# An attention and feed-forward block: sixteen weight loads change queue, one read-back gets a condition, and a turn's tensor step is issued first

## The chip, the cores and the metric

The kernel runs on one core of one Trainium2 chip. The metric is the device time of one execution in microseconds (us). A core has five engines that work side by side, each through its own instructions in a fixed order, and they wait for one another through semaphores: TensorE (PE) multiplies matrices into PSUM, VectorE (DVE) and ScalarE (ACT) do elementwise work and reductions, GpSimd (POOL) does slower elementwise work, and SyncE (SP) mostly issues DMA transfers. A DMA is issued by one of SyncE, ScalarE or GpSimd, in the order of that engine's instructions; an issue that has to wait holds back everything behind it on the same engine.

## The reference

The input is x with 4 batches of 1024 tokens of 256 numbers. Attention has 16 heads of 16 numbers; then a gated feed-forward part with ternary weights follows. All is in 32-bit floats.

```python
q, k, v = split_heads(layernorm(x) @ Wqkv.T)          # 16 heads of 16
s = q @ k.T / sqrt(16)
e = exp(clip(s - max(s), -50, 50))
attn = e / (sum(e) + 1e-6)
x = x + layernorm((attn @ v) @ Wout.T)

h = silu(lin(layernorm(x), w1)) * lin(layernorm(x), w2)   # 256 -> 1024
h = gelu(lin(h, h1)); h = gelu(lin(h, h2))                # 1024 -> 1024
x = x + layernorm(lin(h, w3))                             # 1024 -> 256
```

The 1e-6 is added to a sum of exponentials that were taken relative to the row's maximum. A kernel that doesn't subtract the maximum first must therefore still know it: it adds 1e-6 times the largest exponential of the row.

## The kernel before

**Tiling of attention.** The 16 heads are taken in 4 groups of 4 (`g`), the 1024 queries in 2 halves of 512 (`h`), the 1024 keys in 8 chunks of 128 (`c`). A *unit* is one batch, group and half; there are 4 x 4 x 2 = 32 of them, one after the other. A unit has 8 chunks of 2 tiles (`u`, two heads each), so 512 tiles in all. For each tile TensorE makes the scores `s` (L534) from two stacked operands `sk` and `sq`, ScalarE takes the exponential into a buffer `e` (L535), and TensorE weighs the values `vaug` with it into `acc` (L542). The buffers `e` are a ring of 8 tiles, so that a new exponential overwrites one that must have been weighed, and looked at by VectorE.

**The maxima.** Along the way VectorE keeps, in `top`, the elementwise maximum over chunks of the exponentials of the first 128 queries (`rise`, L554). A query of that kind may have a sum so small that the 1e-6 counts. At a unit's end (`unit_end`) `acc` is transposed into `o` (L787, two buffers), and `divide` (L567 to L587) brings the maxima to the right place: `top` is sent to DRAM as `top_d` (L572), read back as `folded` (`back`, L575, one buffer), reduced by three VectorE instructions (`fold`, L579 and L580), and then `run` takes the last maximum (L584) and calls `quotients`, which divides (L561 to L565) and writes the result to `on`. `run` frees `folded`. For the first group of a later batch, `run` waits until the projection of the batch before has read the same `on`.

**The stacks.** A head group's operands are put together by 32 DMA copies of 64 KB (`stack` and `copies`, L482), 16 for `sk` and then 16 for `sq`, all from SyncE's queue, four in a step. Two groups of stacks exist; the copies for group g + 2 begin when group g has ended and have to land before group g + 1 has.

**Other transfers in attention.** `load_rest` (L218 to L234) lists what is loaded beside the first units: a part of x, then the output weights `wo_sb` in 16 pieces of 16 x 256 (16 KB), then the last batch's x and the scales, one per turn and all from SyncE's queue. The output weights are first read by the projection `py` at the end of batch 0. GpSimd rounds the feed-forward weights (`round_weights`, `round_corners`) with loads and stores on its own queue, copies the values into `vaug` (L512), and takes reciprocal square roots (`rstd`, L107).

**The planner.** The Python code that writes the program runs *turns*. In each, three tiles of scores and exponentials are issued, then maxima of complete chunks, then weighings, then more exponentials, and at the end `side.take`: that spends what is left of the turn on side work, which is the next batch's normalisation, transposes and projections, stack copies, divisions, the ends of batches, and loads. Side work stands in *chains* of `Step`s in `self.first` (divisions and batch ends) and `self.rest` (all else). A step has a gap in turns to its forerunner, a condition `ready`, and a flag `tensor` if it uses TensorE; at most one tensor step is issued in a turn. The order of issue in the turn is the order of the chains. A tensor step issues its matmuls and also the instructions that empty its PSUM tile: `to_vector` (L327), the second half of a projection (L394), `bound` (L426), or the splitting of a transposed input (L327 and L901). All of them write to one PSUM buffer, `misc`, so that the next tensor step's matmuls wait until the last one's tile has been emptied.

**Order on an engine.** What the Python code issues first is first on its engine; there is no reordering afterwards.

Of the kernel before, what the change touches and what calls it, by code (L numbers as in the profile page):

```python
# [21 lines left out]
DH = 16  # L22
# [21 lines left out]
@with_exitstack  # L44
def tile_attention_ffn_block(ctx: ExitStack, tc: tile.TileContext, x, wqk, wv, wo, w1, w1s, w2, w2s, h1, h1s, h2, h2s, w3, w3s, out):

    nc = tc.nc
    B, S, D = x.shape
    bad = ctx.enter_context(tc.tile_pool(name="flag", bufs=1)).tile([1, 1], I32, name="bad")
    tile_fast(tc, x, wqk, wv, wo, w1, w1s, w2, w2s, h1, h1s, h2, h2s, w3, w3s, out, bad)
    failed = nc.values_load(bad[0:1, 0:1], min_val=0, max_val=1 << 24)
    with tc.If(failed > 0):  # L70
        tile_general(tc, x, wqk, wv, wo, w1, w1s, w2, w2s, h1, h1s, h2, h2s, w3, w3s, out)
# [58 lines left out]
def tile_fast(ctx: ExitStack, tc: tile.TileContext, x, wqk, wv, wo, w1, w1s, w2, w2s, h1, h1s, h2, h2s, w3, w3s, out, bad):  # L130
    nc = tc.nc
# [25 lines left out]
    def load_x(b, halves=range(NH)):  # L157
        view = x[b].rearrange("(t p) d -> p t d", p=P)
        for h in halves:
            for at, tokens in pieces(h, view):  # L160
                nc.sync.dma_start(out=xs[b][:, at, :], in_=tokens)
# [34 lines left out]
    with ExitStack() as actx, ExitStack() as rctx:  # L196
# [4 lines left out]
        wo_sb = aw.tile([P, DC, D], F32, name="wo_sb")  # L201
# [16 lines left out]
        def load_rest():  # L218


            def load(out, in_):
                return lambda: nc.sync.dma_start(out=out, in_=in_)

            def load_half(b, h):
                return lambda: load_x(b, [h])

            rest = [load_half(2, h) for h in range(NH)]
            for c in range(DC):
                for h in range(HPT):
                    r = SLOT * (HPT * c + HPG * (h % GPT) + h // GPT)  # L230
                    rest.append(load(wo_sb[DH * h : DH * (h + 1), c, :], wo[r : r + DH, :]))
            rest += [load_half(b, h) for b in range(3, B) for h in range(NH)]
            rest += [load(scales[name], w) for name, w in (("w1", w1s), ("w2", w2s), ("h1", h1s), ("h2", h2s))]
            return rest + [load(w3s_sb, w3s.partition_broadcast(P))]  # L234
# [21 lines left out]
        work = actx.enter_context(tc.tile_pool(name="work", bufs=2, side="right"))  # L256
# [299 lines left out]
        def quotients(g, h, em, o):  # L556

            o = o.rearrange("p (j s) -> p j s", s=SLOT)
            den = small.tile([P, NQ // SLOT], F32, tag="den", name="den")
            n = P // SLOT  # L560
            nc.vector.scalar_tensor_tensor(den[:, 0:n], em, SM_EPS, o[:, 0:n, DH], ALU.mult, ALU.add)  # L561
            nc.vector.tensor_copy(den[:, n:], o[:, n:, DH])
            nc.vector.reciprocal(den, den)
            e = DH * (g % GPT)
            nc.vector.tensor_mul(on[h][:, g // GPT, :, e : e + DH], o[:, :, 0:DH], den.unsqueeze(2).to_broadcast([P, NQ // SLOT, DH]))  # L565

        def divide(g, h, o, top):  # L567


            there = shuffle.tile([HPG, P, P], F32, tag="top", name="top_d")  # L570
            folded = work.tile([P, P // SLOT, P], F32, tag="folded", name="folded", bufs=1)
            nc.sync.dma_start(out=there.rearrange("i k q -> k i q"), in_=top.rearrange("p u n q -> p (u n) q"))  # L572

            def back():
                nc.sync.dma_start(out=folded, in_=there.rearrange("i (k s) q -> (i k) s q", s=P // SLOT))  # L575

            def fold():
                for n in (2, 1):
                    nc.vector.tensor_max(folded[:, 0:n], folded[:, 0:n], folded[:, n : 2 * n])  # L579
                nc.vector.transpose(folded[:, 1], folded[:, 0])  # L580

            def run():
                em = small.tile([P, P // SLOT], F32, tag="em", name="em")
                nc.vector.tensor_reduce(em, folded[:, 1].rearrange("p (j k) -> p j k", k=SLOT), AX.X, ALU.max)  # L584
                quotients(g, h, em, o)

            return [Step(back, 2, False), Step(fold, 2, False, work=1.2), Step(run, 1, False, work=1.4)]  # L587

        def divide_last(g, h, o, top):

# [88 lines left out]
        class Side:  # L679
# [34 lines left out]
            def take(self, room=math.inf, spare=0.0):  # L714

                self.slot += 1
                free, heavy = True, False
                step = self.next_tensor(self.slot)

                self.room = min(self.room, 0.5) + room - (step.work if step and not step.heavy else 0)  # L720
                for chain in self.first + self.rest:
                    while (step := self.due(chain, self.slot, free)) and (step.tensor or not step.work or self.room > spare):
                        chain[0].pop(0)
                        chain[1] = self.slot
                        if step.split:
                            step.run(0)
                            chain[0].insert(0, Step(lambda run=step.run: run(1), 1, work=step.work))
                            self.open = chain
                        else:
                            if step.tensor and self.open is chain:  # L730
                                self.open = None
                            step.run()
                        free = free and not step.tensor
                        heavy = heavy or step.heavy
                        self.room -= 0 if step.tensor else step.work
                self.tired = heavy
# [47 lines left out]
        def unit_end(b, g, h):  # L784

            o = both.tile([P, NQ], F32, tag="o", name="o", bufs=2)
            nc.vector.transpose(o, accs[b, g, h])  # L787
            unit = side.add((divide_last if (b, g) == (B - 1, NG - 1) else divide)(g, h, o, tops[b, g, h]), True)
            if b and not g:

# [382 lines left out]
        class Checks:  # L1173
# [7 lines left out]
            def load(self):  # L1181
                k = self.loaded
                if k < min(len(self.blocks), self.seen + 2):
                    w, c, i = self.blocks[k]
                    self.st[k] = xs[0][:, TPQ * (k % 2) : TPQ * (k % 2 + 1), :].rearrange("p t d -> p (t d)")
                    nc.sync.dma_start(out=self.st[k].rearrange("p (i d) -> p i d", i=i), in_=w[c * P : (c + i) * P, :].rearrange("(i p) d -> p i d", p=P))
                    self.loaded += 1
# [156 lines left out]
        side.add(early + v[2:] + [Step(slots(0, 0), 0, False), Step(slots(0, 1), 0, False)] + sum(qk[1], []) + [Step(lambda: later.update(qk1=0, v=0), 0, False), Step(lambda: add_flags(flags[0] + flags[1]), 0, False)])  # L1344
        begin(0)
        side.add(stack(0, 1) + few(load_rest(), 1))
        side.add([s for k in blocks for s in round_weights(*k)] + [s for k in corners for s in round_corners(*k)])
        made = seen = weighed = half = 0
# [8 lines left out]
        while weighed < len(tiles):  # L1357
# [14 lines left out]
            while halves and weighed + 2 <= n:  # L1372
                b, g, h, c, _ = tiles[weighed]
# [264 lines left out]
```

## Time and profile before

Three runs took 1228.26, 1232.06 and 1233.94 us; the median is 1232.06.

| What | Value |
|---|---|
| Time of the profiled execution | 1232.08 us |
| Its span, first to last instruction | 1230.2 us |
| TensorE's mean granted clock over it | 0.987 |
| Attention stage, roughly | 0 to 592 us |
| TensorE busy in 30 to 600 us | 539.0 of 570 us |
| ScalarE busy in 30 to 600 us | 501.0 of 570 us |
| VectorE busy in 30 to 600 us | 402.4 of 570 us |
| GpSimd busy in 30 to 600 us | 173.4 of 570 us |
| DMA engines, mean share in 30 to 600 us | 0.62 |
| Exponentials (L535) | 512 of 1.043 us, 483.1 us |
| One maximum (L554) | 0.723 us |
| One load of `wo_sb`, issue to landing, median | 2.5 us |

How to read it: "busy" is the time in which an engine executes, "waits" are idle times of an engine, each put down to what ended it. The granted clock is the share of full speed that TensorE's clock was given. In a timeline each row has a start, a length, the work with its tiles (out<-in) and shape, how many instructions were merged into the row, and in brackets the idle time before it and its releaser. SPq rows are SyncE's queue; their length includes waiting in the issue.

### The profile page before, as it was taken

The numbers are of one execution on the slowest core, as the hardware profiler recorded it, in microseconds if no ns is written. First come the engines' busy times: TensorE is split into PE (matmuls) and PEld (weight loads), VectorE is DVE, ScalarE is ACT, GpSimd is POOL, SyncE is SP. The second block draws the span as 40 slices with busy tenths as digits, with TensorE's granted clock in tenths as the row PEclk, the third lists the DMA queues.
The fourth block names the chain that finished last, engine by engine and source line by source line (L and its number), as shares of the span: only waits on it lengthen the run. The fifth ranks groups of instructions, "written<-read, shape, count | busy, mean of one in ns | idle before, by whom it ended". The sixth has DMA issues, their size and how long they took to land.

```text
span 1230.2 us, 21266 instructions
## 1 busy us (share of the span) xinstructions
PE 1169.1 (95%) x7994; PEld 710.1 (58%) x7994; DVE 841.5 (68%) x1500; ACT 885.1 (72%) x1049; POOL 209.1 (17%) x279
## 2 busy tenths in 40 slices
PE   7999999999999999999999999999999999999993
PEld 2333333333333333333578888887888878888783
DVE  3485668777687756868685756867578676784755
ACT  3798899878988989999457565576656766566651
POOL 6222035434354432000000000000000000000000
PEclk8999999999999999999999999999999999999997
DMA  4676755756666666453314341344512545125401
GB/s 132 175 183 152 172 148 134 186 135 175 152 162 154 173 168 148 96 140 128 104 34 138 119 156 52 103 171 147 178 59 97 175 156 176 62 82 199 155 7 37
DMA packets 78672, 163.66 MB, mean 133 GB/s; under 512 B 14688, under 2 KB 40928, under 8 KB 78560
## 3 DMA queue, kind: packets, MB, share of 16 engines
q1 hardware_dynamic: 68624, 131.27, 38.7%
q0 software_dynamic: 9408, 30.42, 7.7%
q8 instruction: 65, 1.06, 0.4%
q10 hardware_dynamic: 528, 0.52, 0.2%
q14 instruction: 47, 0.39, 0.1%
HBM read 98.71 MB, written 29.88 MB: 105 GB/s over the span
## 4 chain that ended last, share of the span: by engine, by line
PE 58%; DVE 12%; ACT 12%; SPq 6%; DMA 6%; issue 5%; ACTq 0%; POOL 0%; POOLq 0%; DVEq 0%
PE ph L1034 27%; PE acc L542 9%; PE pg L955 8%; ACT e L535 6%; PE s L534 6%; SPq L482 5%; PE p L321 3%; DVE lo L929 2%; ACT hi L925 2%; PE py L321 2%; DVE top L554 1%; DMA sq<-cq1lo 1%; DMA folded<-top_d 1%; PE pz L1139 1%; DVE w L1045 1%
## 5 line engine op out<-in xcount | busy, mean ns | idle before, releaser
L535 ACT ACTIVATE e<-s 128x1024 f32<-128x1024 f32 x512 | 483.1, 1043 | 53.8 <-PE s L534 44.1
L542 PE MATMUL acc<-e,vaug 128*32 128x512 f32 (+1 forms) x2424 | 258.7, 539 | 2.9 <-POOL vaug L512 2.9
L534 PE MATMUL s<-sq,sk 64*128 64x512 f32 x1024 | 189.3, 446 | 25.3 <-ACT e L535 17.1
L534 PEld LDWEIGHTS s<-sq,sk 64*128 64x128 f32 x1024 | 87.6, 185 | 172.0 <-ACT e L535 142.1
L1034 PE MATMUL ph<-hi,sq 128*128 128x512 f32 x448 | 178.1, 398 | 0.8 <-DVE w L1045 0.8
L1034 PE MATMUL ph<-lo,sq 128*128 128x512 f32 x448 | 176.7, 394 | 0.0
L1034 PE MATMUL ph<-hi,sk 128*128 128x512 f32 x448 | 176.7, 394 | 0.0
L1034 PE MATMUL ph<-lo,sk 128*128 128x512 f32 x448 | 176.4, 394 | 0.0
L107 POOL TENSOR_TENSOR rstd<-ve,minus_half 128x4 f32<-128x4 f32 (+1 forms) x34 | 38.2, 1123 | 740.6 <-DVE ve L105 681.8
L554 DVE TENSOR_TENSOR top<-top,e 128x512 f32<-128x512 f32 x192 | 138.9, 723 | 24.3 <-ACT e L535 18.5
L542 PEld LDWEIGHTS acc<-e,vaug 128*32 128x32 f32 x2424 | 61.8, 109 | 120.5 <-issue 107.8
L929 DVE TENSOR_TENSOR lo<-c,hi 128x1024 fp32r<-128x1024 f32 x48 | 58.4, 1223 | 66.0 <-ACT hi L925 66.0
L929 DVE TENSOR_TENSOR lo<-g,hi 128x1024 fp32r<-128x1024 f32 x48 | 58.8, 1226 | 58.0 <-ACT hi L925 57.7
L1034 PEld LDWEIGHTS ph<-hi,sq 128*128 128x128 f32 x448 | 84.2, 188 | 21.6 <-DVE w L1045 2.1
L1034 PEld LDWEIGHTS ph<-hi,sk 128*128 128x128 f32 x448 | 84.1, 188 | 20.0
L1034 PEld LDWEIGHTS ph<-lo,sk 128*128 128x128 f32 x448 | 84.1, 188 | 19.9
L1034 PEld LDWEIGHTS ph<-lo,sq 128*128 128x128 f32 x448 | 84.2, 188 | 19.1
L1022 ACT ACTIVATE c<-ph,h_scale 128x512 f32<-128x512 f32 x64 | 40.6, 685 | 50.1 <-PE ph L1034 50.1
L321 PE MATMUL p<-xT,wqk_sb 128*32 128x512 f32 x512 | 69.3, 622 | 4.7 <-ACT wqk_sb L209 2.6
L957 ACT ACTIVATE sg<-pg,w_scale 128x512 f32<-128x512 f32 x64 | 43.6, 688 | 35.7 <-PE pg L955 31.9
L1139 PE MATMUL pz<-w_sb,lo 128*128 128x256 f32 x256 | 61.6, 284 | 2.8 <-DVE lo L929 2.8
L958 DVE SCALAR_TENSOR_TENSOR g<-pg,w_scale,sg 128x512 f32<-128x512 f32 x64 | 47.7, 747 | 23.1 <-ACT sg L957 23.0
(183 smaller groups left out, 1735.1 us busy)
## 6 DMA issues: line engine op xcount, KB each, us to landing
sq<-h_f SPq DMA_DIRECT2D x56, 512.0 KB, 3.8
sk<-h_f SPq DMA_DIRECT2D x56, 512.0 KB, 4.5
w<-in_h_dram POOLq DMA_DIRECT2D x32, 256.0 KB, 5.2
h_f<-wr POOLq DMA_DIRECT2D x16, 512.0 KB, 4.3
x<-in_h_dram SPq DMA_DIRECT2D x16, 512.0 KB, 3.6
top_d<-top SPq DMA_DIRECT2D x30, 256.0 KB, 2.5
folded<-top_d SPq DMA_DIRECT2D x30, 256.0 KB, 3.2
h_f<-wr POOLq DMA_DIRECT2D x16, 384.0 KB, 3.7
```

Of the source, the lines that this page charges most:

```text
L321: nc.tensor.matmul(o[j : j + SLOT, :], w[:, j : j + SLOT], i, **flags)
L482: queue.dma_start(out=stacks[w, i, u][o : o + DH, c0:c1].bitcast(F32), in_=cq[w, m, k][r : r + DH, c0:c1].bitcast(F32))
L534: nc.tensor.matmul(s[:, a, :], stacks[1, g % 2, u][r, c * P : (c + 1) * P], stacks[0, g % 2, u][r, h * NQ : (h + 1) * NQ], start=True, sto ...
L535: nc.scalar.activation(pair(k)[:, u], s, AF.Exp)
L542: nc.tensor.matmul(acc[SLOT * i : SLOT * (i + 1), q0:q1], vaug[g % 2][:, c, i, :], pair(k)[:, i // 2, i % 2, q0:q1], start=c == 0 and q0 = ...
L554: nc.vector.tensor_max(top, top if c > 1 else pair(k - 2)[:, :, :, 0:P], pair(k)[:, :, :, 0:P])
L929: nc.vector.tensor_sub(self.lo[i].t, self.raw[i].t, self.hi[i].t.bitcast(F32))
L955: nc.tensor.matmul(p[:, k, :], homes[n][d][:, m * P : (m + 1) * P], half[:, d, :], start=d == j == 0, stop=d == DC - 1 and j == 1)
L957: nc.scalar.activation(sg, p[:, 0, :], AF.Silu, scale=scales["w1"][:, m : m + 1])
L958: nc.vector.scalar_tensor_tensor(x[i, h][c // 2].t[:, c % 2, :], p[:, 1, :], scales["w2"][:, m : m + 1], sg, ALU.mult, ALU.mult)
L1034: nc.tensor.matmul(p[:, j, :], w, half, start=start and c == n == 0, stop=c == HC // 2 - 1 and n == 1, skip_group_check=True,)
L1139: nc.tensor.matmul(p[:, j, :D], half[:, (t0 + j) * P : (t0 + j + 1) * P], homes["w3"][c], start=c == order[0] and n == 0, stop=c == order[ ...
```

## The change

There are three edits.

1. The 16 loads of the output weights go out on GpSimd's queue. Their place in the list and the turn in which they are issued stay.
2. The reading back of a unit's maxima (`back`) becomes due only when as many divisions have been issued as units were begun before it, that is, when its predecessor's division has been issued.
3. In `take`, chains whose next step is a tensor step are looked at first, then all chains in the order they had.

```diff
-            def load(out, in_):
-                return lambda: nc.sync.dma_start(out=out, in_=in_)
+            def load(out, in_, queue=nc.sync):
+                return lambda: queue.dma_start(out=out, in_=in_)
...
-                    rest.append(load(wo_sb[DH * h : DH * (h + 1), c, :], wo[r : r + DH, :]))
+                    rest.append(load(wo_sb[DH * h : DH * (h + 1), c, :], wo[r : r + DH, :], nc.gpsimd))
...
+        divided = {"made": 0, "done": 0}
+
         def divide(g, h, o, top):
...
+            mine = divided["made"]
+            divided["made"] += 1
...
                 quotients(g, h, em, o)
-
-            return [Step(back, 2, False), Step(fold, 2, False, work=1.2), Step(run, 1, False, work=1.4)]
+                divided["done"] += 1
+
+            begun = Step(back, 2, False)
+            begun.ready = lambda: divided["done"] == mine
+            return [begun, Step(fold, 2, False, work=1.2), Step(run, 1, False, work=1.4)]
...
-                for chain in self.first + self.rest:
+                chains = self.first + self.rest
+                for chain in [c for c in chains if c[0] and c[0][0].tensor] + chains:
                     while (step := self.due(chain, self.slot, free)) and (step.tensor or not step.work or self.room > spare):
                         chain[0].pop(0)
                         chain[1] = self.slot
```

Where instructions come to stand in the two programs, engine by engine:

| Engine | What moves |
|---|---|
| TensorE | nothing |
| SyncE | the 16 weight loads are gone; one read-back (L575, batch 1, group 1, first half) stands behind eight stack copies instead of before them |
| GpSimd | 16 more DMA issues, from the second batch's `rstd` on; one `rstd` behind a weight load |
| VectorE | in some 35 places the emptying of a PSUM tile stands before a fold, a division, or small work instead of behind it; that one unit's fold and division come about a unit later |
| ScalarE | two instructions in the feed-forward part change places |

## The prediction

> **What bounds the kernel now.** I read the busy times first, then TensorE's own waits over the attention stage, then the timeline around each long one.
>
> ```profile
> PE 1169.1 (95%) x7994; PEld 710.1 (58%) x7994; DVE 841.5 (68%) x1500; ACT 885.1 (72%) x1049; POOL 209.1 (17%) x279
> ```
>
> TensorE (PE) is busy for 95% of the 1230.2 us span, so all that can go is its idle time and the time in which its clock is halved. The change touches attention alone, about 0 to 592 us. TensorE's waits there from 44 us on, when the first values are in place (total us, number, longest):
>
> ```profile
> PE s L534 <- ACT e L535: 17.1, 50, 1.8
> PE s L534 <- DMA sq<-cq1lo: 7.4, 5, 2.9
> PE py L321 <- DVE norm L426: 2.4, 2, 2.1
> ```
>
> The first row is fifty waits for exponentials, and no edit removes an exponential. The other two rows are few and long. TensorE's timeline (start, length, work, idle before it):
>
> ```profile
> 101.67 0.95 PE L534 MATMUL s<-sq,sk 64*128 64x512 f32 x2 [2.86 <-DMA sq<-cq1lo]
> 102.56 2.33 PE L542 MATMUL acc<-e,vaug 128*32 128x256 f32 x16
> 104.82 1.65 PE L534 MATMUL s<-sq,sk 64*128 64x512 f32 x6
> ...
> 248.60 0.47 PE L534 MATMUL s<-sq,sk 64*128 64x512 f32 x1 [2.79 <-DMA sq<-cq1lo]
> 249.85 2.79 PE L542 MATMUL acc<-e,vaug 128*32 128x512 f32 x16
> 252.57 0.97 PE L363 MATMUL pt<-ident,xn 128*128 128x128 f32 x4
> ...
> 345.95 1.93 PE L321 MATMUL py<-wo_sb,oT 128*32 128x256 f32 x32 [2.13 <-DVE norm L426]
> ```
>
> These are three stalls, and the matmuls behind the first two are slow: from start to next start, the six score matmuls at 104.82 take 1.57 us where 0.89 is usual, and the sixteen weighings at 249.85 take 2.72 where 1.85 is usual. The table by windows gives a granted clock of 0.78 over 98.8 to 106.5, 0.77 over 245.8 to 253.3, and 1.00 around 345.
>
> **Part 1: output weights on GpSimd's queue.** The first stall waits for the last stack copies of head group 2, batch 0. SyncE's queue before it (each row: start, time in the queue):
>
> ```profile
> 88.81 3.11 SPq L482 DMA_DIRECT2D sq<-cq1lo  x4
> 92.02 0.53 SPq L572 DMA_DIRECT2D top_d<-top  x1
> 92.59 0.55 SPq L222 DMA_DIRECT2D wo_sb<-in_wo_dram  x1
> 93.19 3.62 SPq L482 DMA_DIRECT2D sq<-cq1hi  x4
> 96.91 0.53 SPq L575 DMA_DIRECT2D folded<-top_d  x1
> 97.49 0.42 SPq L222 DMA_DIRECT2D wo_sb<-in_wo_dram  x1
> 97.96 2.41 SPq L482 DMA_DIRECT2D sq<-cq1lo  x4
> ```
>
> The queue issues without a pause, and seven weight loads stand in it between 74.4 and 98.0 us. From start to next start they take 0.48, 0.68, 0.62, 1.61, 0.62, 0.60 and 0.47 us, 5.1 in all. About 1.1 of the 1.61 looks like a full DMA system (engines 94% busy over 84 to 88 us) and may return on the next copy, so 4.0 to 5.1 us come free. Nothing else holds the queue: the maxima that L572 sends were ready at 84.4. The last copy was issued until 100.37 and landed 1.7 us later. It would now land at about 97.0 to 98.1, and TensorE wants it at 98.8. So the stall goes, **2.86 us**.
>
> On GpSimd the sixteen loads cost an issue of 0.54 to 0.79 us each by its own rows, some 10 us. GpSimd idles 23.5 us in one wait (84.1 to 107.6) just there, the copy of the next values has a whole head group to spare, and the first reader of the weights is the projection at 193.8. Cost: nothing. Here a rule speaks against the change: the Trainium skill, page "DMA: Bandwidth & Descriptors", section "SWDGE vs HWDGE vs iDMA", wants plain transfers on SyncE or ScalarE, since GpSimd builds descriptors in software (first byte about 1 us instead of 0.6, by the same page). If each load ended a wait, that would be an estimated 16 x 0.4 = 6.4 us lost. By the rows nobody waits for these loads, and I take 0.
>
> The same queue makes TensorE wait 0.76 us at 138.85. Four more weight loads leave ahead of that (2.3 us), but the queue then meets the maxima of the next unit, ready only at 122.2, and loses nearly all of it again. I count nothing there.
>
> **Part 2: read-back only after the predecessor's division.** On SyncE this moves exactly one read-back, past eight stack copies:
>
> ```profile
> 231.53 3.36 SPq L482 DMA_DIRECT2D sq<-cq1lo  x4
> 241.93 0.33 SPq L575 DMA_DIRECT2D folded<-top_d  x1
> 242.31 2.41 SPq L482 DMA_DIRECT2D sq<-cq1hi  x4
> 244.76 2.49 SPq L482 DMA_DIRECT2D sq<-cq1lo  x4
> ```
>
> L575 sits in the queue from 234.9 to 241.9 because the buffer `folded` is held by the unit before, whose division waits for a projection. The eight copies behind it need 4.9 us and TensorE wanted them at 245.8. Ahead of L575 they are issued by 239.8 and land about 242: the stall of **2.79 us** goes. The new wait is a planner's condition and blocks no queue; what is late next is that unit's division, by some 15 us. Its reader is the projection at the batch's end, over 50 us on, and its output buffer `o` is wanted again only at 271.7, so the price is nothing. On GpSimd one `rstd` of the same batch end slips behind two load issues (1.4 us); it too feeds nothing that is due.
>
> **The clock.** The Trainium skill, page "TensorE: Matmul & The Clock Gate", section "Part 1: The HAM clock gate", lets the clock fall to half after at least one idle window of about 3.4 us. By that rule neither stall could cost clock, and the two would be worth 2.86 + 2.79 = 5.65. The trace differs: 0.78 and 0.77 follow stalls of 2.86 and 2.79. From the slow rows, the second lost 2.72 - 1.85 = 0.87 on weighings and 0.91 - 0.59 = 0.32 on transposes, 1.2 us; the first 1.57 - 0.89 = 0.68 on scores and an estimated 0.4 to 0.9 on mixed weighings, about 1.3. I follow the rows: **4.2 and 4.0 us** for the two.
>
> **Part 3: the tensor step first.** TensorE's order doesn't change by a single instruction; what moves is VectorE's. In some 35 places the emptying of a PSUM tile (L327, L394, L426, L901) passes a fold (about 1.05 us), a division (about 1.3) or small work. At 341.81 the tile `pn` was ready, but VectorE did division and statistics from 342.6 and reached L426 at 345.2. Now L426 follows the transpose L787 directly. That transpose itself may slip by 0.7, since its forerunners wait too; L426 then ends near 344.2 instead of 345.9. Gain **1.7 us** of 2.13.
>
> The other sign: where the tile isn't ready, VectorE now idles with the fold or division behind it, and the next maximum comes later by up to the work passed, 0.6 to 1.6 us. An exponential overwrites what a maximum reads, so it may wait. I set each delay against the distance between the maximum's end and the exponential that reuses its buffer: most have 1.5 us or more, and two in mid-stage fall short, by 0.4 and 0.1 us, where ScalarE is not what TensorE waits for. One place has none:
>
> ```profile
> 576.20 0.69 DVE L327 TENSOR_SCALAR ck1hi<-fpt 128x512 fp32r<-128x512 f32 x1 [1.57 <-PE fpt L898]
> ...
> 584.93 5.60 ACT L535 ACTIVATE e<-s 128x1024 f32<-128x1024 f32 x6 [2.70 <-DVE top L554]
> ```
>
> VectorE idles 1.57 us here after a division of 1.3 (573.3 to 574.6). The division now comes behind the idle time and everything up to 584.8 shifts, so TensorE's stall of 1.79 at 586 grows: **-1.2 us**. It can be 1.3, the whole division, or 0 if VectorE catches up before 584.8.
>
> **Sum.** 4.2 + 4.0 + 1.7 - 1.2 = 8.7, less 0.3 for the short places: 8.4 us. The profiled execution took 1232.08 (span 1230.2), the median of the runs is 1232.06; the sum applies to either. **1223.7 us.**
>
> **Rivals.**
> - *Part 1 only half works.* If the queue is held by the DMA engines (share 0.6 to 0.9 there) and not by issue time, the copies land as late as before. For: the first copy at 93.19 took 1.7 us alone. Against: rows of 0.5 us all around. Then the 4.2 stay lost: 1228.
> - *The waits reappear.* The copies for group 3 stall instead of those for group 2, and what TensorE gains it spends on ScalarE, busy 501 of 570 us in 30 to 600. For: fifty waits for exponentials. Against: ScalarE idled together with TensorE in all three stalls. 1231.
> - *VectorE becomes the wait, slower than before.* Place: the maxima behind emptyings that wait for TensorE. Price: about 1 us per place, 35 places; the gains of 9.9 are eaten when more than a quarter of the places reach TensorE. For: a maximum only 0.1 to 0.6 us ahead of its exponential in seven cases. Against: in the whole stage ScalarE waits for a maximum only 2.9 us, and VectorE is 71% busy. At half of the places, 17.5 - 9.9: 1239.7.
> - *The order isn't what the words say.* True for TensorE, as told; it is inside the forecast.
>
> **Numbers.** Forecast 0.60, half of part 1 0.17, reappearing 0.11, VectorE 0.12. The forecast's own range is 1220.5 (all 2.13 and the 0.76 too, no cost at 586) to 1226.5. To leave out no more than two in ten it reaches from 1218.5 (with 2 us of scatter) to 1231.5. About 0.5%, 6.2 us, is what a measurement here can tell from no change: faster is under 1225.9, slower over 1238.2. Faster 0.64 (nearly all of the forecast, some of the half), same 0.25 (the rest of the half, reappearing, a mild VectorE), slower 0.11 (VectorE).
>
> **What would show it.** Right: no wait of `s` for a copy of `sq` over 1 us near 99 and 246 us, a granted clock of 1.00 there, no idle time before `py` near 340, weight loads in GpSimd's rows. Wrong: a stall of over 2 us for a copy somewhere between 95 and 250, more than 6 us of ScalarE waiting for maxima, or a wait at 580 that grows past 3.5 us.

## The result, and the profile after

Twenty runs of the changed kernel, taken alternately with twenty of the kernel before, gave:

| | before | after |
|---|---|---|
| Median of 20 runs (range), us | 1229.9 (1226.4 to 1233.9) | 1227.0 (1223.1 to 1232.3) |
| Profiled execution, us | 1232.08 | 1231.73 |

The ratio is 0.9982, with a 95% interval of 0.9968 to 0.9995: times the median of before that is 2.2 us less (the two medians differ by 2.9), with a forecast of 8.4. By the 0.5% that the prediction named, that is no change. Part of the distance from the forecast time lies in its base: the profiled execution of before took 2.2 us more than the median of these twenty. The profiled execution of after took 4.8 us more than its own median, so its trace shows more time handed back than a usual run loses.

The busy times of after:

```profile
PE 1167.6 (95%) x7994; PEld 710.5 (58%) x7994; DVE 841.2 (68%) x1500; ACT 884.6 (72%) x1049; POOL 214.8 (17%) x295
```

TensorE is busy for 1.5 us less than before, and the span is 0.3 us shorter (1229.9). TensorE's waits in after from 44 to 592 us (total us, number, longest):

```profile
PE s L534 <- ACT e L535: 18.8, 51, 2.9
PE s L534 <- DMA sq<-cq1lo: 3.6, 2, 2.1
PE s L534 <- DMA sq<-cq0lo: 1.6, 2, 1.3
PE acc L542 <- DVE o L796: 1.2, 2, 1.0
PE s L534 <- issue: 1.2, 1, 1.2
PE py L321 <- DVE bounds L452: 1.2, 1, 1.2
PE pn L424 <- DVE sq L402: 0.6, 1, 0.6
```

Before, three rows held most of it. Now `py` no longer waits for `norm`, and the copies cost 5.2 us instead of 7.4. But three rows are new in which TensorE waits for VectorE: for `o`, `bounds` and `sq`. These are not the maxima and exponentials that the prediction examined.

The three stalls of the prediction are gone. In the table by windows of after, TensorE is busy throughout, and its granted clock stands third from the right, at 1.00 in all three:

```profile
95.00:107.00 12.00, 11.71 (x94) 4.68 (x92) 10.30 (x22) 11.40 (x13) 2.98 (x5) 1.00 0.27 59
240.00:253.00 13.00, 13.00 (x114) 4.76 (x110) 9.65 (x23) 12.21 (x15) 6.04 (x8) 1.00 0.30 74
338.00:347.00 9.00, 8.94 (x88) 3.30 (x80) 8.66 (x21) 8.50 (x11) 5.94 (x6) 1.00 0.69 188
```

What came in their place stands in TensorE's timeline (start, length, work, idle before it):

```profile
134.96 1.27 PE L534 MATMUL s<-sq,sk 64*128 64x512 f32 x4 [2.13 <-DMA sq<-cq1lo]
171.48 0.38 PE L424 MATMUL pn<-sq,heads_bf 128*32 128x512 bf16 x1 [0.62 <-DVE sq L402]
212.54 1.92 PE L542 MATMUL acc<-e,vaug 128*32 128x512 f32 x16 [1.03 <-DVE o L796]
279.60 0.47 PE L534 MATMUL s<-sq,sk 64*128 64x512 f32 x1 [1.16 <-issue]
281.57 1.64 PE L534 MATMUL s<-sq,sk 64*128 64x512 f32 x5 [1.50 <-DMA sq<-cq1lo]
283.15 3.64 PE L542 MATMUL acc<-e,vaug 128*32 128x512 f32 x16
376.68 1.93 PE L321 MATMUL py<-wo_sb,oT 128*32 128x256 f32 x32 [1.16 <-DVE bounds L452]
585.40 0.50 PE L534 MATMUL s<-sq,sk 64*128 64x512 f32 x2 [2.87 <-ACT e L535]
```

The sixteen weighings at 283.15 last 3.64 us where those at 212.54 last 1.92: the granted clock is at half for 6.8 us around them (280.65 to 287.47). TensorE issues the same 7994 matmuls in the same order in both programs, so the same matmul can be looked up in both traces. After is ahead of before by 0.9 us at 76 us, 5.1 at 101, 3.0 at 171, 8.3 at 244, 2.4 at 287, 4.7 at 341, 1.5 at 377 and 0.6 at 585. The 0.9 us at 76 are a remainder of the first 44 us, where the traces differ by 1.4 us in clock and waits, and not a gain of an edit. The gains came in the places forecast, and in this execution nearly all was handed back between and behind them, 6 us of it at the copies near 281.

### The profile page after: what moved, and what is told of

Same layout as the page of the kernel before. It is cut to its first block, busy times and chain, and to the rows that moved or that the text cites. A ratio compares the mean times of both kernels' runs of the same rounds, so it can differ in the third digit from the quotient of the medians.

```text
span 1229.9 us, 21278 instructions
## 1 busy us (share of the span) xinstructions
PE 1167.6 (95%) x7994; PEld 710.5 (58%) x7994; DVE 841.2 (68%) x1500; ACT 884.6 (72%) x1049; POOL 214.8 (17%) x295
## 4 chain that ended last, share of the span: by engine, by line
PE 60%; ACT 13%; DVE 12%; issue 5%; DMA 4%; SPq 4%; ACTq 0%; POOL 0%; POOLq 0%; DVEq 0%
PE ph L1043 27%; PE acc L542 10%; PE pg L964 9%; ACT e L535 8%; PE s L534 6%; SPq L482 3%; PE p L321 3%; DVE lo L938 2%; ACT hi L934 2%; PE py L321 2%; DVE top L554 2%; PE pz L1148 1%; DVE w L1054 1%; DMA folded<-top_d 1%; PE pv L321 1%
## 5 line engine op out<-in xcount | busy, mean ns | idle before, releaser
L534 PE MATMUL s<-sq,sk 64*128 64x512 f32 x1024 | 189.6, 446 | 26.3 <-ACT e L535 18.8
```

The lines of the kernel that those rows point to most:

```text
L534: nc.tensor.matmul(s[:, a, :], stacks[1, g % 2, u][r, c * P : (c + 1) * P], stacks[0, g % 2, u][r, h * NQ : (h + 1) * NQ], start=True, sto ...
```

## The experiments

All were timed beside the kernel before on the same chip. Ratios are to it, in brackets the 95% interval; a change in us is the ratio's distance from 1, times the median of before.

**Each edit alone, and the first two together.** The three kernels with one edit each have that part of the diff shown above and nothing else. The fourth has the first two, with the loop of `take` as before:

```diff
-                chains = self.first + self.rest
-                for chain in [c for c in chains if c[0] and c[0][0].tensor] + chains:
+                for chain in self.first + self.rest:
```

Edit 1 alone:

> The kernel before with the first edit alone (output weights on GpSimd's queue). Theory 'given back at the copies': the wait of TensorE for a copy of sq near 99 us (2.86 us) and the halved clock behind it go, TensorE is 4 to 5 us ahead at 110 us, and then 1 to 2 us of it come back at 135 us, where the copies of the next group are late; the stalls at 246 and 344 us stay. Time: 1 to 4 us below before. Theory 'VectorE is the wait': this edit touches no VectorE order, so all of 4 us stays to the end.

Edit 2 alone:

> The kernel before with the second edit alone (read-back after the predecessor's division). Both theories: the stalls at 99 and 344 us stay, the one at 246 us (2.79 us) and its halved clock go, TensorE is about 4 us ahead at 256 us. 'Given back at the copies': 1 to 3 us of it are lost at a later group's copies (near 285 us or 350 us), time 1 to 3 us below before. 'VectorE is the wait': 4 us below before.

Edit 3 alone:

> The kernel before with the third edit alone (tensor step first). The wait before py at 344 us goes (2.1 us). 'VectorE is the wait': TensorE meets new waits on VectorE (near 172, 212, 377 us, and 1.1 us more at 585 us), about 4 us in all, so the edit alone costs 1 to 3 us. 'Given back at the copies': the new waits on VectorE come only when TensorE is ahead; the edit alone is within 1 us of before.

Edits 1 and 2:

> The first two edits without the third. 'VectorE is the wait': faster than all three together, by 2 to 4 us, so 5 to 7 us below before. 'Given back at the copies': TensorE is about 8 us ahead at 256 us, loses 3 to 5 us at the copies near 285 and 355 us, and the time is 2 to 4 us below before, as with all three.

| Kernel | Median, us (before: 1230.96) | Ratio | Change, us |
|---|---|---|---|
| edit 1 | 1229.03 | 0.9988 [0.9979, 0.9998] | -1.5 |
| edit 2 | 1225.16 | 0.9958 [0.9942, 0.9973] | -5.2 |
| edit 3 | 1233.66 | 1.0035 [1.0017, 1.0053] | +4.3 |
| edits 1 and 2 | 1221.81 | 0.9941 [0.9922, 0.9961] | -7.2 |

The changes add up: -7.2 and +4.3 make -2.9, where all three together measured -2.2. So the first two edits together do nearly what was forecast for them (edit 1 less, edit 2 more), and the third costs time. TensorE's waits over the same stage with edits 1 and 2:

```profile
PE s L534 <- ACT e L535: 17.4, 50, 1.8
PE s L534 <- DMA sq<-cq1lo: 1.9, 2, 1.4
PE py L321 <- DVE norm L426: 1.6, 1, 1.6
PE pt L363 <- DVE xT L327: 0.2, 1, 0.2
```

and with edit 3 alone (rows of DMA and VectorE from 0.5 us up):

```profile
PE s L534 <- DMA sq<-cq1lo: 5.5, 3, 2.9
PE acc L542 <- DVE o L788: 1.4, 3, 1.0
PE pn L424 <- DVE sq L402: 1.1, 1, 1.1
PE s L534 <- DMA sq<-cq0lo: 0.7, 1, 0.7
PE py L321 <- DVE bounds L452: 0.5, 1, 0.5
```

The rows for `o`, `sq` and `bounds` come with edit 3 and only with it. Edit 1 has a price of its own: without the stall at 99 us TensorE reaches the next group's copies earlier, and the wait there grows. TensorE in before, then with edit 1 alone:

```profile
138.85 0.46 PE L534 MATMUL s<-sq,sk 64*128 64x512 f32 x1 [0.76 <-DMA sq<-cq1lo]
```
```profile
134.92 1.24 PE L534 MATMUL s<-sq,sk 64*128 64x512 f32 x4 [1.77 <-DMA sq<-cq1lo]
```

Along the common order of matmuls edit 1 gains 4.0 us at 99 us, as forecast, and loses 1.0 here. Another 1.1 goes near 246, where a stall as long as in before (2.76 us) is followed by 6.8 us of half clock instead of 3.4. Edit 2 gains all of its 5.2 us between 240 and 249.

**Is it GpSimd's transfers?** After's stall at 281 us stood where GpSimd stores and loads feed-forward weights (the DMA engines are 91% busy over 274 to 278 us). So before, after, and the kernel with edits 1 and 2 were each run without those transfers: the square layers' weights are not loaded, rounded values not stored, and other data is read in their place.

```diff
-                for j in range(2):
-                    nc.gpsimd.dma_start(out=st["w"]..., in_=rows[:, j])
+                nc.gpsimd.memset(st["w"], 1.0)
...
-                nc.gpsimd.dma_start(out=factors[n]..., in_=r...)
+                pass
```

Before, without the transfers:

> The kernel before, with GpSimd's transfers for the square weights left out: their loads are a memset, their stores are gone, and the factor loads of the feed-forward part read other data of the same size, so the square layers are computed with wrong weights. This takes some 15 MB off the DMA engines between 150 and 480 us. 'Given back at the copies': the stall at 99 us stays (it lies before these transfers), that at 246 us stays (a held queue, not a slow transfer), that at 344 us stays; the short waits near 390 us go. 1 to 3 us below before.

After, without the transfers:

> The changed kernel with the same transfers left out, in the same way. 'Given back at the copies' (copies land late because GpSimd's transfers share the DMA engines): the stalls near 281 and 354 us and the halved clock there go, and the distance to quiet_before is 6 to 9 us, two to three times what the change gains with the transfers. 'VectorE is the wait': the distance stays at 2 to 3 us, with the waits near 172, 212, 377 and 585 us in place.

Edits 1 and 2, without the transfers:

> The first two edits with GpSimd's transfers for the square weights left out as in quiet_before and quiet_after (the square layers are computed with wrong weights). If edit 3 costs through VectorE's order alone, this is 3 to 5 us faster than quiet_after (1222.7 us), so near 1218. If edit 3 costs only because the shifted copies meet GpSimd's transfers, it is like quiet_after or slower, 1222 to 1226.

| Without the transfers | Median, us | Ratio |
|---|---|---|
| before | 1232.96 | 1.0010 [0.9995, 1.0025] |
| edits 1 and 2 | 1226.59 | 0.9959 [0.9941, 0.9976] |
| all three | 1222.74 | 0.9926 [0.9903, 0.9950] |

Before did not get faster without the transfers, against 1 to 3 us expected, and after's distance from it, 10 us, is more than either theory allowed. Between the last two rows edit 3 gains some 4 us (1226.59 to 1222.74, on two chips; the intervals just overlap). By the traces it removes two waits of `py` for `norm` (1.76 and 1.62 us) and one of `pv` (0.84), and it costs some 0.5 before `pn`, 0.5 and 0.6 before `acc` and 1.1 at 581; the stalls for copies at 281 and 354 us don't come. So the waits for VectorE come without the transfers too, but there is more for edit 3 to remove, and no stall for copies. The two profiled executions are 1.0 us apart (1229.02 and 1228.03), so they show only a part of the 4. Leaving the transfers out also changes what VectorE and GpSimd have to wait for, and with it the places where edit 3 bites; what the transfers themselves do to its price is not shown.

**Which tensor steps.** Both kernels have edits 1 and 2. In one only the step `bound`, whose tile `pn` is emptied by L426 into `norm`, is put first (it is marked `early`); in the other all tensor steps but that one. (The tile `bounds`, for which `py` waits above, comes from another step, `flag`.)

```diff
+                    flags[m][-1].early = True
...
-                for chain in self.first + self.rest:
+                chains = self.first + self.rest
+                lead = [c for c in chains if c[0] and c[0][0].tensor and self.due(c, self.slot, free)][:1]
+                for chain in [c for c in lead if c[0][0].early] + chains:
```

The other has `not c[0][0].early`.

Only `bound` first:

> The first two edits, and the tensor step first only where it is the bound's (its tile pn is emptied by L426, and was ready when VectorE came to it at five of its seven moved places). TensorE's order is that of before. Theory 'VectorE is the wait' (edit 3 costs where an emptying that is not ready yet is put ahead of other work): the wait before py near 340 us goes (1.6 to 2.1 us) and none of the waits near 172 (sq), 212 (o) and 377 us (bounds) come, nor the longer one near 585; 8 to 10 us below before, about 2 below the first two edits alone. Rival 'any change of the order costs by shifting copies against GpSimd's transfers': 2 to 5 us below before, like all three.

All others first:

> The complement: the first two edits, and the tensor step first except where it is the bound's. 'VectorE is the wait': the waits near 212, 377 and 585 us are there, the wait before py near 340 us too; 5 to 7 us above the first two edits alone, so 0 to 2 us below before. Rival 'shifting copies': as f_bound_first, 2 to 5 us below before.

Only `bound`: 1222.32 us, 0.9934 [0.9909, 0.9960]. All others: 1231.19, 1.0000 [0.9988, 1.0011]. The whole price is in the others. The one wait that I had seen edit 3 remove, that of `py` for `norm`, is gone in the first kernel and still there in the second (2.1 us). Against edits 1 and 2 alone (0.9941) the gain of the first cannot be told from nothing.

**A lighter SyncE queue.** The wait at 135 us is for copies that stand in SyncE's queue among loads of x and of scales. Three kernels put these loads on GpSimd's queue too. They have edits 1 and 2 and, of edit 3, the step `bound` alone, all, or nothing:

```diff
-    def load_x(b, halves=range(NH)):
+    def load_x(b, halves=range(NH), queue=nc.sync):
...
-                return lambda: load_x(b, [h])
+                return lambda: load_x(b, [h], nc.gpsimd if b == 3 else nc.sync)
...
-            rest += [load(scales[name], w) for ...
+            rest += [load(scales[name], w, nc.gpsimd) for ...
```

`bound` alone:

> f_bound_first with the last batch's x and the scales on GpSimd's queue too, so that SyncE's queue carries four to eight issues less between 104 and 139 us. If the wait of 0.8 to 2.1 us for a copy of sq near 135 us is a matter of issue time, as the one at 99 us was, it goes and the time is 1 to 3 us below f_bound_first. If it is held by the maxima that the queue waits for, it stays.

All of edit 3:

> All three edits, and beside them the last batch's x and the four scales on GpSimd's queue, so that SyncE issues fewer transfers between 100 and 145 us; nothing else is changed. Theory (edit 3's price is mainly VectorE's: what VectorE hands over to pn, acc, the tile behind bounds and the last division comes later, wherever the copies stand): ratio 0.994 to 0.997 to the kernel before, and some 3 to 5 us slower than the kernel that differs from it in having only the bounds first (0.9900); stalls of 0.5 to 1.5 us near 172, 212 and 377 us and 2.9 us near 580 as before. Rival (the price is mainly that of copies that come into GpSimd's transfers, and goes with a lighter queue): ratio 0.989 to 0.992, no stall for a copy of sq over 0.6 us, and the VectorE stalls under 2 us together.

None of it:

> Edits 1 and 2, and the last batch's x and the four scales on GpSimd's queue, without any part of edit 3. It is the base for the two kernels that have all of edit 3 (this call) or its bounds alone (0.9900) with the same queues. Theory: edit 3's good part is the one stall before py near 340 us (1.6 to 2.1 us), so the ratio is 0.991 to 0.993, and the kernel with all of edit 3 is 1 to 4 us slower than this one. Rival (with the copies out of the way edit 3 gains): this kernel is slower than the one with all of edit 3, by 1 to 4 us.

| With the loads on GpSimd's queue | Median, us | Ratio |
|---|---|---|
| edits 1 and 2 | 1220.19 | 0.9915 [0.9889, 0.9942] |
| the same, `bound` first | 1217.16 | 0.9900 [0.9872, 0.9929] |
| the same, all of edit 3 | 1226.71 | 0.9963 [0.9945, 0.9981] |

The middle one beats both kernels of this case, by 12.3 us against before and about 10 against after, though its interval overlaps that of the first. Its waits over the stage are down to two rows:

```profile
PE s L536 <- ACT e L537: 18.4, 54, 1.8
PE pt L364 <- DVE xT L328: 0.3, 1, 0.3
```

That kernel is 5.2 us below the one with `bound` first and the old queue (1222.32), where 1 to 3 were expected. First and last row were timed side by side: edit 3 costs 6.5 us there, more than the 1 to 4 expected. Part of that is clock: the mean granted clock of the runs is 0.9901 with edit 3 and 0.9920 without, an estimated 0.0019 x 1220 = 2.3 us, good to about 1 us by the scatter of the runs. The two traces show the rest, since little else differs. Each VectorE row gives start, length and work, with the idle time before it in brackets. With all of edit 3, near 171 us:

```profile
168.18 0.69 DVE L394 SCALAR_TENSOR_TENSOR cq1lo<-p,cq1hi 128x512 fp32r<-128x512 f32 x1 [3.84 <-ACT cq1hi L324]
168.78 1.54 DVE L584 TENSOR_TENSOR folded<-folded 128x256 f32<-128x256 f32 x2
170.36 0.31 DVE L585 STREAM_TRANSPOSE folded<-folded 128x128 f32<-128x128 f32 x1
170.60 0.65 DVE L402 TENSOR_TENSOR sq<-ck0hi 128x512 bf16<-128x512 f32 x1
```

and without it:

```profile
162.70 0.75 DVE L584 TENSOR_TENSOR folded<-folded 128x256 f32<-128x256 f32 x2
163.48 0.31 DVE L585 STREAM_TRANSPOSE folded<-folded 128x128 f32<-128x128 f32 x1
163.72 0.65 DVE L402 TENSOR_TENSOR sq<-ck0hi 128x512 bf16<-128x512 f32 x1
166.62 0.69 DVE L394 SCALAR_TENSOR_TENSOR cq1lo<-p,cq1hi 128x512 fp32r<-128x512 f32 x1 [2.25 <-ACT cq1hi L324]
```

The same four pieces of work. Without edit 3 VectorE folds and squares, and idles afterwards. With it the emptying L394 is first in line, VectorE idles 3.84 us for ScalarE's part of the same tile, and the fold that was ready stands behind it. So `sq` is late as well, and TensorE waits for it, which it doesn't in the other kernel:

```profile
171.30 0.38 PE L424 MATMUL pn<-sq,heads_bf 128*32 128x512 bf16 x1 [1.20 <-DVE sq L402]
```

The stall for copies at 280 us has the same root, by way of SyncE. With all of edit 3, VectorE and SyncE:

```profile
251.67 0.69 DVE L394 SCALAR_TENSOR_TENSOR ck0lo<-p,ck0hi 128x512 fp32r<-128x512 f32 x1 [0.53 <-ACT ck0hi L324]
252.28 0.28 DVE L589 TENSOR_REDUCE em<-folded 128x4 f32<-128x128 f32 x1
```
```profile
252.59 0.33 SPq L580 DMA_DIRECT2D folded<-top_d  x1
252.95 1.14 SPq L482 DMA_DIRECT2D sk<-ck1hi  x2
```

and without it:

```profile
247.56 0.27 DVE L589 TENSOR_REDUCE em<-folded 128x4 f32<-128x128 f32 x1
...
248.83 0.68 DVE L394 SCALAR_TENSOR_TENSOR ck0lo<-p,ck0hi 128x512 fp32r<-128x512 f32 x1
```
```profile
247.87 0.33 SPq L580 DMA_DIRECT2D folded<-top_d  x1
248.23 1.89 SPq L482 DMA_DIRECT2D sk<-ck1hi  x2
```

The read-back L580 waits for the buffer that L589 frees, and goes out 0.03 us after the reduction's end in one kernel and 0.04 in the other. With edit 3 the reduction stands behind L394. TensorE is 3.5 us later in the kernel with edit 3 at that point, but L580 is 4.72 later: 1.2 us are lost, and the rest of the group's copies stand behind L580. The last of them is issued 4.70 us later and takes 0.4 us more to land. TensorE waits for it, first with all of edit 3, then without:

```profile
280.18 0.96 PE L534 MATMUL s<-sq,sk 64*128 64x512 f32 x5 [1.55 <-DMA sq<-cq1lo]
```
```profile
275.09 0.96 PE L534 MATMUL s<-sq,sk 64*128 64x512 f32 x5 [0.23 <-DMA sq<-cq1lo]
```

So the theory's ratio came true (0.9963), and the rival's did not (0.989 to 0.992): a lighter SyncE queue does not take the price away. Step by step along TensorE's common order, edit 3 costs about 1.2 us before `pn`, 1.0 before `acc` (212 us), 1.3 at the copies (280), 0.5 at those near 349, 0.7 before `py` behind `bounds` (371) and 1.1 at 580, and it gains 1.9 before `py` at 338. That makes 3.9 of the 6.1 us between the two profiled executions. The half clock behind the stalls cancels between these two: 3.4 us each at 334 and 577 in the kernel without edit 3, 6.8 at 580 in the other. Another 1.6 is a longer wait at 134 us (2.19 against 0.63), which I can't lay on edit 3: the read-back there waits for a transfer, with the buffer long free.

## Why the prediction was right and wrong

**Part 1** was right in what goes and short in what comes. The stall at 101.67 and its slow clock went, worth 4.0 us in the place. The loads land later from GpSimd's queue (a median 4.1 us after issue in after, 2.5 in before), but nothing waits for them. "I count nothing there", said of the 0.76 us at 138.85, was wrong: that wait grew to 1.4 to 2.9 us in every kernel that has edit 1 and the old queue for x and the scales, alone or with others. Of the 4.2 us forecast 1.5 were measured (0.2 to 2.6 by the interval). The wait accounts for 1.0 of the 2.7 that are missing; in the one trace 1.1 more are half clock at 246, but 1.6 come back at 585, where half clock stays away, so the rest is open.

**Part 2** was right in its mechanism and a little small: 5.2 us measured for 4.0 forecast. A second, short wait for the last copy goes with the first, together some 3.6 us, and the slow clock cost some 1.6 instead of 1.2. No price for the late division showed anywhere. Together with part 1 it is 7.2 for 8.2; that the sum comes so near is luck, since the two errors offset each other.

**Part 3** is the step that failed: forecast as a gain of 0.2 us (1.7 - 1.2 - 0.3), measured as a loss of 4.3 alone and about 5 behind the other two. The gain was there (2.3 us at 341 in after, for 1.7), and the loss at 585 was sized well (1.08, for 1.2). What failed is "I set each delay against the distance between the maximum's end and the exponential that reuses its buffer". That is one consumer of VectorE's late work, and VectorE has at least four more: the squares for `pn`, the transpose that frees `acc`, `bounds`, which empties the PSUM tile that `py` needs, and the reduction that frees `folded`, behind which SyncE's copies stand. In the pair with the lighter queue they lost 1.2, 1.0, 0.7 and 1.3 us. Such waits also bring half clock, an estimated 2.3 us there. The sum had "less 0.3 for the short places"; by the measured loss it should have been less 5.

**The rivals.** "VectorE becomes the wait" had the right mechanism. It named the maxima as the place, but ScalarE waits only 5.3 us for maxima in after (2.9 before), under the 6 that were to count against me. A handful of places of 1 us in the 35 were enough to lose part 3, fewer than the quarter that the rival wanted to be decisive; the total stayed faster since parts 1 and 2 outweighed it. "The waits reappear" was right on group 3's copies at 135 us (2.13 us, over the 2 us named as a sign against the forecast), and wrong about the reason: TensorE's gain was not spent on ScalarE, whose exponentials cost 18.8 us for 17.1, with 1.08 of that at 585. "Part 1 only half works" would have had the copies at 99 us land late; they didn't. "The order isn't what the words say" doesn't matter for the outcome.

**What stays open.** Why edit 3 gains without GpSimd's transfers is only in part accounted for. Nor is it settled what sets the wait at 135 us, which was between 0 and 2.9 us in kernels that differ little there. And I have no run that repairs the four consumers one at a time; the price of each is read from the two traces, not from a kernel.

## What to carry to other kernels

When an instruction is moved up on an engine with a fixed order, ask whether its input is ready there: if it isn't, everything that it passes now waits for that input, and each consumer of each passed instruction has to be looked at, on other engines and in DMA queues too, not only the one that the stage is known to wait for. A wait inside a queue of transfers (the read-back here, 7 us in the queue) costs what stands behind it; issuing it behind eight other copies gained 5.2 us. Test edits that came together one at a time: two of these three made 7 us, and the third hid it.

## What the runs showed of the hardware

A stall of some 2 to 3 us is followed by half clock in some executions and not in others. The wait of 1.78 us near 575 us was followed by 6.8 us of half clock in the kernel with only `bound` first, and by none in the kernel with edits 1 and 2; behind after's 2.13 us at 135 there was none, and 6.8 us of it behind its 1.16 and 1.50 at 280.

Where the stall falls explains most of this. In each of the fourteen traces the granted clock changes only at times that lie whole multiples of 3.41 us apart (in before at 103.08, 106.50, 249.86 and 253.27). I divided the time from 44 to 1190 us into these stretches and took TensorE's idle time, by the modelled ends of its matmuls, in each that ran at full clock. Of 4618 stretches with under 1.2 us idle none was followed by half clock; of 36 with 1.2 to 2.0 us, 13 were; of 14 with 2.0 us or more, all. The rows below give a stretch, its length, PE's busy time, and, third from the right, the granted clock. With only `bound` first the wait falls into one stretch, which is idle for 1.85 us:

```profile
572.99:576.41 3.42, 1.57 (x18) 0.45 (x10) 3.28 (x6) 1.64 (x2) 0.00 (x0) 1.00 0.00 0
576.41:579.82 3.41, 2.94 (x16) 1.17 (x20) 2.14 (x4) 3.41 (x5) 0.00 (x0) 0.50 0.01 2
```

With edits 1 and 2 the same wait is split over two, idle for 1.36 and 1.25 us (the stretches are counted back from that trace's one change, at 1200.73), and the clock stays:

```profile
569.27:572.68 3.41, 2.05 (x22) 0.60 (x18) 3.32 (x7) 0.72 (x2) 0.00 (x0) 1.00 0.00 0
572.68:576.10 3.42, 2.17 (x18) 0.98 (x22) 2.60 (x5) 3.42 (x5) 0.00 (x0) 1.00 0.00 0
```

After's 2.13 us at 135 is split in the same way (1.0 and 1.2 us idle), while 1.74 us before 280.65 lie in one stretch. Between 1.2 and 2.0 us the traces do not tell what decides.

Half clock for 6.8 us costs a busy TensorE up to 3.4 us (an estimate, half of it), so a stall's cost can differ by as much between two executions of nearly the same program. Much of the spread of one kernel goes with the clock: among the 27 runs of before timed beside the last two kernels the mean granted clock is 0.982 in two that took 1235.1 and 1235.7 us, and 0.991 in the two fastest (1226.0). A single profile can show where a stall is, and not what it is worth to 1 us.
